# A two-layer decoder on one core: the last pairs of tiles of layer 2's expert loop put under conditions, its attention biases computed earlier, queries scaled on eviction, the residual added in the matmul

## The chip, the core and the metric

The kernel runs on one core of one Trainium2 chip. The core has a matmul engine (PE, with its weight loads listed apart as PEld), a vector engine (DVE), an activation engine (ACT), GpSimd (POOL) and a sync engine (SP); each works through its own list of instructions in order. In this kernel SP issues all plain transfers, and POOL issues the indirect ones, which scatter rows to listed places in DRAM or add rows there. The metric is the device time of one execution in microseconds. A profile is one such execution, recorded by the hardware profiler.

## The reference

Two layers, each a cross-attention and a mixture of experts, over x of 8 x 256 tokens of width 256 (2048 tokens), with a context of 8 x 120 rows:

```python
x = x + L0_xattn(layernorm(x), ctx, ctx, mask, w_q, w_k, w_v, w_o)      # 16 heads of 16, masked
x = x + L0_ffn(layernorm(x), ...)       # 64 experts, 8 per token, at most 128 tokens each, and a shared one
x = x + L1_xattn(layernorm(x), ctx, W_q, b_q, W_k, b_k, W_v, b_v, W_o, b_o)   # no mask, biases
x = x + L1_ffn(layernorm(x), ...)       # 32 experts, 6 per token, no limit; a shared one; 16 anchors
...
_, topidx = jax.lax.top_k(masked, TOP_K)                # 6 of 32 experts, from 2 of 4 groups
lg = topidx[:, 0] // (E // L)                           # one of 16 anchors, from the first expert
routed = jnp.einsum('te,teh->th', cw, eo)               # each expert: silu(x g) * (x u), then down
out = routed + shared + ANCHOR_ALPHA * anchor
```

Scores are divided by 4, the root of the head size. How many tokens fall to an expert or an anchor of layer 2 depends on the data; nothing limits it.

## The kernel before

**Order.** The program is unrolled. Attention and routing are written as tasks with an engine, an estimated duration and what they read and write; a planner (`Plan.run`) picks the task that can start first by its own estimates, with a rank, and so fixes each engine's list when the program is built. The expert loops (`expert_pairs`) are written out in a fixed order, with leftover tasks of the plan put between them (`beside`) in layer 1. Every engine instruction of these goes through the helper at L61, so the profile's groups have this line and are told apart by their tiles.

**Layer 1** runs attention and routing interleaved (two tiles of 128 tokens a unit of routing); POOL scatters each token's row to the lists of its 8 experts (`rows_f`, L237). Then 32 pairs of experts run: load the rows (`xg`), transpose (`xgp`), gate and up (`eg`), down (`eo`), weighting on ACT (`ye`), and POOL adds each half-pair to one of three accumulators in DRAM (`acc_f`, in the helper at L61). The experts' weights come in groups of four, six groups in buffers (`NEW`, L46).

**Layer 2's attention** begins at L328 with its biases: three small loads (`bc`, `br`, `bv`), the key bias split by the two halves of the heads (`bk`), and the value bias carried through the output weights (`bvs`, `bvp`) into `br`. Keys (`keys`, L357) and values (`values`, L376) are computed for all batches; each PSUM result is evicted in two parts, one by DVE and one by ACT, into KT and V. Then per pair of token tiles: `fetch` (L1229) loads layer 1's three partial sums and DVE adds them to x (`x_sb<-x_sb,sum_acc_f`), `queries` (L391) normalises, transposes and projects, and POOL adds `br` to x. Per tile `unit` (L422) computes the scores of 8 heads at a time; DVE takes the maxima and multiplies them by -0.25 (`mx_a<-mx_a`); ACT computes exp(0.25 s + m); PE transposes, weights the values, projects (`pj`); DVE adds the projection to x. Layer 1's units are the same with a mask, which DVE applies first (`pr_a<-sc_a,topm`).

**Layer 2's experts.** Tokens are sorted into tiles of 128 rows while routing runs: an expert gets a new tile whenever its last is full (`tiles`, L1040), so an expert with n tokens holds n/128 tiles, rounded up, numbered without gaps. `ntile` has each expert's count of tiles, and `own` which expert has which tile. There is room for 128 routed and 32 anchor tiles (L32), the most that can be needed. `ffn1` (L1116) goes through them in pairs, the 16 pairs of anchor tiles first, then the 64 routed pairs, all of them whatever the data: a tile that no expert took holds blank rows, is worked through with expert 0's weights, and its rows are added to spare rows of the accumulators. The number of each tile's expert is read from `which` into a register of PE. Last, `collect` (L269) loads the three accumulators by pieces of 256 tokens, DVE adds them to x, and SP stores the result.

**Buffers that tie this.** SP runs five pairs ahead with the rows; `yring` (L1128) holds four weighted pairs until their adds have landed, so ACT waits for adds and POOL for ACT.

Of the kernel before, what the change touches and what calls it, by code (L numbers as in the profile page):

```python
# [34 lines left out]
EPS = 1e-5  # L35
MASKED = -4.0e9
PAD = -3.0e38
# [7 lines left out]
EARLY = 2  # L45
NEW = 6  # L46
NRING = 7
NACC = 3

# [116 lines left out]
def decoder_kernel(ctx: ExitStack, tc: tile.TileContext, x, ctxT, mask, aw0, aw1, bqk, bvo,  # L166
# [20 lines left out]
    w_a0 = attention_weights(0, aw0)  # L187
    mi = const.tile([P, 2, SK], I32, tag="mi", name="mi")
    nc.sync.dma_start(mi, mask.rearrange("(t p) k -> p t k", p=P))
# [15 lines left out]
    nc.vector.tensor_reduce(par, hm.rearrange("p (q two) -> p two q", two=2), AX.X, ALU.add)  # L205

    side = const.tile([P, 2, QR], F32, tag="side", name="side")
    nc.vector.memset(side, 0.0)
    for q in range(2):
        nc.vector.memset(side[:, q, q * DH : (q + 1) * DH], 1.0)  # L210
    before = const.tile([P, P], F32, tag="before", name="before")
# [106 lines left out]
    def attention(layer, w, route, share):  # L318
# [9 lines left out]
        if layer:  # L328
            bc = w1.tile([P, 2, KD], F32, tag="bc", name="bc")
            nc.sync.dma_start(bc, bqk)  # L330

            bk = w1.tile([P, KD, 2], F32, tag="bk", name="bk")
            vector.tensor_tensor(bk, bc[:, 1].unsqueeze(2).to_broadcast([P, KD, 2]),
                                 par.unsqueeze(1).to_broadcast([P, KD, 2]), ALU.mult)
            br = w1.tile([P, D], F32, tag="br", name="br")
            nc.sync.dma_start(br, bvo[1:2, :].partition_broadcast(P))
            bv = w1.tile([P, KD], F32, tag="bv", name="bv")
            nc.sync.dma_start(bv, bvo[0, :].rearrange("(k p) -> p k", p=P))

            bvs = w1.tile([P, KD, P], F32, tag="bvs", name="bvs")  # L340
            vector.tensor_copy(bvs, bv.unsqueeze(2).to_broadcast([P, KD, P]))
            ps = ps_m.tile([P, D], F32, tag="m", name="bvp")
            for k in range(KD):
                tensor.matmul(ps, bvs[:, k, :], w[:, 3, k, :], start=(k == 0), stop=(k == KD - 1))
            vector.tensor_tensor(br, br, ps, ALU.add)
        else:
            m01 = w1.tile([P, 2, SK], F32, tag="m01", name="m01")
            vector.tensor_scalar(m01, mi, 0.0, None, ALU.not_equal)

            top = w1.tile([P, 2, SK], F32, tag="top", name="topm")  # L350
            vector.tensor_scalar(top, m01, BIG, MASKED, ALU.mult, ALU.add)

# [4 lines left out]
        def keys(m, c, rank):  # L357
            ps = m_tile([P, HB], f"kp_{n}_{m}_{c}")

            def product():  # L360
                for k in range(KD):
                    ins = tensor.matmul(ps(), w[:, 1, k, m * P : (m + 1) * P], cT[:, k, c * HB : (c + 1) * HB],
                                        start=(k == 0), stop=(k == KD - 1))
                return ins
            add("PE", 1.7, product, [], [ps], rank)
            dst = lambda q: KT[:, m, q, c * HB : (c + 1) * HB]
            bias = lambda q: bk[:, m, q : q + 1] if layer else 0.0
            add("DVE", 0.8, lambda: vector.tensor_scalar(dst(0), ps(), par[:, 0:1], bias(0), ALU.mult, ALU.add),
                [ps], [("K", layer, m, 0, c)], rank)
            add("ACT", 0.75, lambda: scalar.activation(dst(1), ps(), AF.Identity, scale=par[:, 1:2], bias=bias(1)),  # L370
                [ps], [("K", layer, m, 1, c)], rank)

# [3 lines left out]
        def values(b, rank):  # L376
# [7 lines left out]
            add("PE", 0.9, product, [], [ps], rank)  # L384
            for q, (e, copy) in enumerate((("DVE", vector.tensor_copy), ("ACT", scalar.copy))):
                split = lambda q=q: ps().rearrange("p (m c q d) -> p m q c d", m=KD, q=2, d=DH)[:, :, q]
# [4 lines left out]
        def queries(b, rank):  # L391
# [16 lines left out]
            def out_():  # L408
                if not layer:
                    return scalar.copy(QT(), ps())  # L410
                for m in range(KD):
                    ins = scalar.activation(QT()[:, m, :], ps()[:, m, :], AF.Identity, bias=bc[:, 0, m : m + 1])
                return ins
# [8 lines left out]
        def unit(i, QT):  # L422
# [3 lines left out]
            for half in range(2):  # L426
# [23 lines left out]
                def maxima(sc=sc, pr=pr, mx=mx):  # L450

                    if layer:
                        vector.tensor_reduce(mx().rearrange("p (c h) -> p c h", c=2), sc(), AX.X, ALU.max)
                    else:
                        vector.tensor_reduce(mx(), pr(), AX.X, ALU.max)
                    return vector.tensor_scalar(mx(), mx(), -0.25, None, ALU.mult)
                add("DVE", 1.32, maxima, [ps if layer else pr], [mx], i)
                pT = plan.tile(w2, [SK, 8, P], "pT", f"pT_{n}_{i}_{half}", 4)
                pTs.append(pT)
                for a in range(2):  # L460
                    c = 2 * half + a

                    def exponentials(sc=sc, pr=pr, mx=mx, a=a, c=c):

                        for h in range(4):
                            head = (h // 2) * HH + 2 * c + h % 2
                            to = pr()[:, 4 * a + h, :]
                            ins = scalar.activation(to, sc()[:, a, h, :] if layer else to, AF.Exp, scale=0.25,
                                                    bias=mx()[:, 4 * a + h : 4 * a + h + 1], accum_out=den()[:, head : head + 1])
# [40 lines left out]
            pj = m_tile([P, D], f"pj_{n}_{i}")  # L510

            def project():
                for k in range(KD):
                    ins = tensor.matmul(pj(), oT()[:, k, :], w[:, 3, k, :], start=(k == 0), stop=(k == KD - 1))
                return ins
            add("PE", 0.85, project, [oT], [pj], i - 0.5)
            add("DVE", 0.42, lambda: vector.tensor_add(x_sb[:, i, :], x_sb[:, i, :], pj()), [pj], [("x", i)], i - 0.5)

# [264 lines left out]
    def ffn0():  # L783
        stack = ExitStack()
        pool = lambda name, bufs, **kw: stack.enter_context(tc.tile_pool(name=f"f0{name}", bufs=bufs, **kw))
        w2, w3 = pool("b2", 2), pool("b3", 5)
        ps_g, ps_o = (pool(f"ps_{c}", 2, space=PSUM) for c in "go")
# [37 lines left out]
        def beside(s):  # L825
            plan.some(4)

        expert_pairs(0, list(range(E0 // 2)), (ps_g, ps_o), load, take,
# [23 lines left out]
    rt0 = f0.enter_context(tc.tile_pool(name="rt0", bufs=2))  # L852
    stack = attention(0, w_a0, route0, shared0)
    plan.run(lambda t: t.late < 1)
    stack.close()
# [260 lines left out]
    def ffn1():  # L1116
# [17 lines left out]

        pe = ps_m.tile([1, NTL], F32, tag="m", name="pe1")
        tensor.matmul(pe, wcol, own, start=True, stop=True)
        which = rt1.tile([1, NTL], I32, tag="ch1", name="which")
        vector.tensor_copy(which, pe)
# [62 lines left out]
        def actT_of(p):  # L1201
            o = 2 * P * (p % 2)
            return aring[0 : width(p), o : o + 2 * P].rearrange("p (j c) -> p j c", j=2)

        expert_pairs(1, [*range(NPR, NPR + NPA), *range(NPR)], (ps_g, ps_o), load, take,
                     lambda p: tring[:, p % 2], si_of, act_of, actT_of, gate_up, down_of, width, finish, lambda s: None, NRING - 2,
                     lambda t, g: scalar.activation(t, g, AF.Silu), False)

# [98 lines left out]
```

## Time and profile before

| | us |
|---|---|
| median of three runs (lowest, highest) | 1100.41 (1093.51, 1100.88) |
| the profiled execution | 1098.8 |
| its span, first to last instruction | 1097.1 |
| busy: PE, POOL, DVE, ACT | 851.0, 637.8, 572.2, 474.4 |
| last scatter of layer 1 issued | 263.7 |
| last add of layer 1's loop issued | 435.6 |
| first scores of layer 2 | 463.2 |
| last scatter of layer 2 issued | 741.5 |
| first and last add of layer 2's loop | 755.7, 1062.9 |

The span in 40 slices of 27 us (each digit the busy share in tenths):

```profile
PE   6989997997997782797979795507988899898710
PEld 4767775786996671565857674306776777777600
DVE  5988885752543341698766856503333433333305
ACT  3987785710231221296957380002333433343310
POOL 2047755564455677342505573673878888887860
PEclk9999996998999896898978986558999999999955
```

Read it by stages: to slice 10 layer 1's attention and routing, to 16 its experts, to 25 layer 2's attention and routing, then PE stops while POOL scatters, and from 28 on layer 2's experts. A busy engine isn't yet the one that sets the time: what counts is which wait ends last in each stage. In the tables by group a row has line, engine, operation, output and inputs, count, then total and mean time, and the idle time before them with what ended it.

### The profile page before, as it was taken

The page shows a single profiled execution, that of the slowest core. Times are in us where ns is not written, and L with a number is a line of the kernel's source. Part 1 is how long each engine was busy: PE and PEld are TensorE (multiplying, and loading weights), DVE is VectorE, ACT ScalarE, POOL GpSimd, SP SyncE. Part 2 cuts the span into 40 slices and gives each one's busy share as a digit, 9 for nine tenths or more (in the row PEclk, how much of TensorE's full clock was granted, in tenths as well). Part 3 has the DMA queues.
Part 4 walks back from the last instruction along what each step waited for, and adds up shares of the span by engine and source line. Part 5 has one row for each costly group of instructions (what it writes and reads, how often), then busy time and mean ns, then how long its engine had stood idle before and what let it go on. Part 6 is the DMA issues. An engine that isn't in the chain of part 4 may idle for free. (4 is left out here: it accounts for less than half of the span.)

```text
span 1097.1 us, 18163 instructions
## 1 busy us (share of the span) xinstructions
PE 851.0 (78%) x5630; PEld 685.5 (62%) x5630; DVE 572.2 (52%) x2025; ACT 474.4 (43%) x1756; POOL 637.8 (58%) x574
## 2 busy tenths in 40 slices
PE   6989997997997782797979795507988899898710
PEld 4767775786996671565857674306776777777600
DVE  5988885752543341698766856503333433333305
ACT  3987785710231221296957380002333433343310
POOL 2047755564455677342505573673878888887860
PEclk9999996998999896898978986558999999999955
DMA  9999999983699977630102222957978888888568
GB/s 319 298 353 277 275 286 257 348 305 97 170 285 324 241 126 105 172 108 30 58 1 72 83 98 103 405 222 199 166 137 145 145 147 147 146 153 137 68 98 270
DMA packets 158509, 202.34 MB, mean 184 GB/s; under 512 B 22343, under 2 KB 139406, under 8 KB 158160
## 3 DMA queue, kind: packets, MB, share of 16 engines
q1 hardware_dynamic: 114640, 144.86, 43.8%
q0 software_dynamic: 43776, 56.33, 28.9%
q8 instruction: 47, 0.77, 0.3%
q14 instruction: 46, 0.38, 0.1%
HBM read 95.19 MB, written 116.63 MB: 193 GB/s over the span
## 5 line engine op out<-in xcount | busy, mean ns | idle before, releaser
L237 POOL DMA_INDIRECT rows_f<-pay,idx x240 | 235.4, 981 | 192.3 <-issue 53.2
L61 POOL DMA_INDIRECT acc_f<-yring,etok x160 | 249.9, 1562 | 73.0 <-ACT yring L61 31.1
L61 POOL DMA_INDIRECT acc_f<-ye,etok x64 | 98.9, 1545 | 70.4 <-ACT ye L61 43.2
L61 ACT ACTIVATE yring<-eo,ewt 128x256 f32<-128x256 f32 x128 | 60.7, 475 | 152.7 <-DMA acc_f<-yring,etok 136.7
L61 PE MATMUL eg<-w,free 128*128 x512 | 121.5, 380 | 0.0
L61 DVE TENSOR_TENSOR free<-sring,eg 128x256 f32<-128x256 f32 (+1 forms) x80 | 31.6, 394 | 169.9 <-ACT sring L61 169.9
L61 ACT ACTIVATE pr_a<-pr_a,mx_a 128x120 f32<-128x120 f32 x256 | 97.9, 392 | 3.2 <-DVE mx_a L61 3.0
L61 PEld LDWEIGHTS eg<-w,free 128*128 128x128 f32 x512 | 92.8, 191 | 10.1
L61 ACT ACTIVATE pr_a<-sc_a,mx_a 128x120 f32<-128x120 f32 x256 | 90.9, 416 | 15.9 <-DVE mx_a L61 15.9
L61 PE MATMUL sc_a<-KT_a,QT_a 32*128 32x240 f32 x512 | 76.0, 427 | 16.1 <-ACT pr_a L61 9.2
L61 PE MATMUL tp_a<-ident,pr_a 128*120 128x128 f32 x512 | 82.9, 293 | 4.9 <-ACT pr_a L61 2.0
L61 ACT COPY pT_a<-tp_a 120x512 f32<-120x512 f32 x128 | 74.0, 614 | 23.9 <-PE tp_a L61 22.9
L61 DVE COPY free<-xgp 128x512 f32<-128x512 f32 x80 | 54.8, 685 | 50.0 <-PE xgp L61 49.8
L61 PE MATMUL xgp<-ident,room 128*128 128x128 f32 x320 | 50.6, 282 | 34.7 <-DMA room<-rows_f 34.5
L61 PEld LDWEIGHTS tp_a<-ident,pr_a 128*120 128x120 f32 x512 | 63.8, 146 | 21.5 <-ACT pr_a L61 10.7
L61 PE MATMUL eo<-w,aring 128*128 x256 | 68.7, 392 | 1.0 <-ACT aring L61 1.0
L61 PEld LDWEIGHTS xgp<-ident,room 128*128 128x128 f32 x320 | 39.8, 145 | 47.0 <-DMA room<-rows_f 34.9
L61 PEld LDWEIGHTS sc_a<-KT_a,QT_a 32*128 32x128 f32 x512 | 47.5, 206 | 33.2 <-ACT pr_a L61 16.1
L61 ACT ACTIVATE ye<-eo,ewt 128x256 f32<-128x256 f32 x64 | 26.9, 471 | 95.2 <-DMA acc_f<-ye,etok 64.6
L61 PE MATMUL eg<-xgT,ew 128*128 128x128 f32 x512 | 67.5, 289 | 0.0
L61 PEld LDWEIGHTS eg<-xgT,ew 128*128 128x128 f32 x512 | 65.4, 207 | 0.2
L61 ACT ACTIVATION_READ_ACCUMULATOR pr_a<-sc_a,mx_a 128x1 f32 x256 | 65.2, 262 | 0.0
(227 smaller groups left out, 1716.6 us busy)
## 6 DMA issues: line engine op xcount, KB each, us to landing
ew<-in_ew SPq DMA_DIRECT2D x16, 1536.0 KB, 9.1
rows_f<-blank SPq DMA_DIRECT2D x5, 4624.0 KB, 46.7
room<-rows_f SPq DMA_DIRECT2D x80, 289.0 KB, 3.5
acc_f<-blank SPq DMA_DIRECT2D x6, 2176.0 KB, 23.2
w<-in_ew SPq DMA_DIRECT2D x8, 1536.0 KB, 19.5
rows_f<-blank SPq DMA_DIRECT2D x2, 5136.0 KB, 44.9
xg<-rows_f SPq DMA_DIRECT2D x32, 321.0 KB, 6.2
sum_acc_f<-acc_f SPq DMA_DIRECT2D x24, 256.0 KB, 2.8
```

What stands on the lines that cost most here:

```text
L61: ins = call(*args, **kw)
L237: ins = nc.gpsimd.indirect_dma_start(out=rows, out_offset=bass.IndirectOffsetOnAxis(ap=idx, axis=0), in_=pay, in_offset=None, **kw)
```

## The change

Six edits. (1) `ffn1` runs 56 routed and 12 anchor pairs always; the rest stands in five blocks under nested conditions (two blocks of two anchor pairs; routed blocks of two, two and four), each entered if the count of tiles in use exceeds what has been worked through. The counts are sums of `ntile` by a matmul next to `pe1`, copied into `which`, and each engine reads them into a register. The blocks call `expert_pairs` anew. (2) Layer 2's biases are loaded during layer 1 into a buffer that the mask leaves free, and computed in step 24 of layer 1's expert loop. (3) Queries are multiplied by 0.25 as they are evicted, in both layers, so that the maxima are negated within the reduction and the multiplication after it falls away. (4) Layer 2's keys and values are evicted by ACT alone. (5) Layer 2's residual is added in PE by an identity matmul into the projection's PSUM, and ACT copies the sum to x; before, DVE added. (6) `NEW` goes from 6 to 7, the two pools of layer 1's loop change places in memory, and an unused constant (`side`) goes.

```diff
+SCALE = 0.25
-MASKED = -4.0e9
+MASKED = -1.0e9
-NEW = 6
+NEW = 7
+SURE = 56, 12
+LEFT = (2, 2, 4), (2, 2)
...
         if layer:
-            bc = w1.tile([P, 2, KD], F32, tag="bc", name="bc")
-            nc.sync.dma_start(bc, bqk)
...
+            bc, bk, br = consts1
...
-            add("DVE", 0.8, lambda: vector.tensor_scalar(dst(0), ps(), par[:, 0:1], bias(0), ALU.mult, ALU.add),
-                [ps], [("K", layer, m, 0, c)], rank)
...
+            for q in range(2):
+                if q or layer:
+                    add("ACT", 0.75, lambda q=q: scalar.activation(dst(q), ps(), AF.Identity, scale=par[:, q : q + 1], bias=bias(q)),
+                        [ps], [("K", layer, m, q, c)], rank)
...
-                    ins = scalar.activation(QT()[:, m, :], ps()[:, m, :], AF.Identity, bias=bc[:, 0, m : m + 1])
+                    ins = scalar.activation(QT()[:, m, :], ps()[:, m, :], AF.Identity, scale=SCALE, bias=bc[:, 0, m : m + 1])
...
-                        vector.tensor_reduce(mx().rearrange("p (c h) -> p c h", c=2), sc(), AX.X, ALU.max)
...
-                    return vector.tensor_scalar(mx(), mx(), -0.25, None, ALU.mult)
+                        return vector.tensor_reduce(mx().rearrange("p (c h) -> p c h", c=2), sc(), AX.X, ALU.max, negate=True)
+                    return vector.tensor_reduce(mx(), pr(), AX.X, ALU.max, negate=True)
...
             def project():
+                if layer:
+                    tensor.matmul(pj(), ident, x_sb[:, i, :], start=True, stop=False)
                 for k in range(KD):
...
+            if layer:
+                add("PE", 1.3, project, [oT, ("x", i)], [pj], i - 0.5)
+                add("ACT", 0.4, lambda: scalar.copy(x_sb[:, i, :], pj()), [pj], [("x", i)], i - 0.5)
+            else:
...
-        w2, w3 = pool("b2", 2), pool("b3", 5)
+        w3, w2 = pool("b3", 5), pool("b2", 2)
...
             plan.some(4)
+            if s == 24:
+                biases()
...
+    nc.sync.dma_start(bc, bqk)
+    nc.sync.dma_start(br, bvo[1:2, :].partition_broadcast(P))
+    nc.sync.dma_start(bv, bvo[0, :].rearrange("(k p) -> p k", p=P))
+
+    def biases():
+
+        vector.tensor_tensor(bk, bc[:, 1].unsqueeze(2).to_broadcast([P, KD, 2]),
+                             par.unsqueeze(1).to_broadcast([P, KD, 2]), ALU.mult)
+        vector.tensor_scalar(bc[:, 0], bc[:, 0], SCALE, None, ALU.mult)
...
+        vector.tensor_copy(bvs, bv.unsqueeze(2).to_broadcast([P, KD, P]))
+        ps = ps_m.tile([P, D], F32, tag="m", name="bvp")
+        for k in range(KD):
+            tensor.matmul(ps, bvs[:, k, :], w_a1[:, 3, k, :], start=(k == 0), stop=(k == KD - 1))
+        vector.tensor_tensor(br, br, ps, ALU.add)
...
+        pe = ps_m.tile([1, NTL + 2], F32, tag="m", name="pe1")
+        tensor.matmul(pe[:, 0:NTL], wcol, own, start=True, stop=True)
+        tensor.matmul(pe[:, NTL : NTL + 2], ntile, kind[:, 0 : NC1 : E1], start=True, stop=True)
...
-        expert_pairs(1, [*range(NPR, NPR + NPA), *range(NPR)], (ps_g, ps_o), load, take,
...
+        def pairs(*order):
+            expert_pairs(1, order, (ps_g, ps_o), load, take, lambda p: tring[:, p % 2], si_of, act_of, actT_of, gate_up,
+                         down_of, width, finish, lambda s: None, min(len(order), NRING - 2),
+                         lambda t, g: scalar.activation(t, g, AF.Silu), False)
...
+        in_use = [nc.values_load(which[0:1, NTL + c : NTL + c + 1], min_val=0, max_val=m, skip_runtime_bounds_check_because="a count")
+                  for c, m in ((0, NRT), (1, NAT))]
+        pairs(*range(NPR, NPR + SURE[1]), *range(SURE[0]))
+
+        def rest(c, p0, at, blocks):
+            if blocks:
+                with tc.If(in_use[c] > 2 * at):
+                    pairs(*range(p0 + at, p0 + at + blocks[0]))
+                    rest(c, p0, at + blocks[0], blocks[1:])
+
+        rest(1, NPR, SURE[1], LEFT[1])
+        rest(0, 0, SURE[0], LEFT[0])
```

## The prediction, made before the changed kernel ran

> **What bounds the kernel now.** I read the page first, then the busy time by stretches, then POOL's order of time in the last third, then the chain of waits, and last the gap between the layers. The page's chain and its two costliest groups there:
>
> ```profile
> DMA 17%; issue 6%; PE 4%; POOL 3%; DVE 1%; ACT 1%; SPq 0%; POOLq 0%; ACTq 0%; DVEq 0%
> L61 POOL DMA_INDIRECT acc_f<-yring,etok x160 | 249.9, 1562 | 73.0 <-ACT yring L61 31.1
> ```
>
> The chain consists mostly of the 160 indirect adds of layer 2's expert loop (80 pairs of tiles, two adds each). Is POOL, which issues them, the bound? The stretches (columns: stretch, its length, then busy time and count of PE, weight loads, DVE, ACT, POOL, then granted clock, DMA share, GB/s):
>
> ```profile
> 800.00:850.00 50.00, 42.63 (x223) 34.24 (x221) 17.33 (x84) 17.55 (x48) 39.45 (x26) 1.00 0.83 142
> 900.00:950.00 50.00, 46.09 (x246) 38.53 (x245) 19.23 (x92) 19.31 (x52) 40.84 (x27) 0.99 0.87 151
> 1050.00:1097.00 47.00, 0.00 (x0) 0.00 (x0) 16.43 (x24) 0.85 (x2) 12.30 (x8) 0.50 0.78 204
> ```
>
> POOL shows 82% busy and PE 92%, so PE looks nearer. The order of time on POOL says otherwise (start, duration, what, idle before it):
>
> ```profile
> 1059.13 1.57 POOL L61 DMA_INDIRECT acc_f<-yring,etok  x1 [0.30 <-issue]
> 1061.01 1.56 POOL L61 DMA_INDIRECT acc_f<-yring,etok  x1 [0.30 <-DMA acc_f<-yring,etok]
> 1062.87 1.57 POOL L61 DMA_INDIRECT acc_f<-yring,etok  x1 [0.30 <-issue]
> ```
>
> Each add takes 1.56 us and 0.30 us follows that nothing can use: a beat of 1.865 us, 3.73 us a pair. From 755.66 (first add) to 1064.44 (end of the last) are 308.8 us; 160 beats are 298.4. So only 10 us of the loop are not POOL's beat, and PE finishes at 1047.2, 17 us before POOL. The loop's length is the number of adds.
>
> After it the chain goes on through landing and collecting:
>
> ```profile
> 1061.01 1.56 POOL acc_f L61
> 1062.87 4.13 DMA acc_f<-yring,etok
> 1067.47 0.41 SPq L275
> ```
>
> The second place is the start of layer 2's attention. DVE there:
>
> ```profile
> 439.68 0.16 DVE L61 TENSOR_TENSOR bk<-bc,par 128x4 f32<-128x4 f32 x1 [19.81 <-DMA bc<-in_bqk]
> 442.26 0.47 DVE L61 COPY bvs<-bv 128x256 f32<-128x256 f32 x1 [2.42 <-DMA bv<-in_bvo]
> 445.17 0.42 DVE L61 TENSOR_TENSOR br<-br,bvp 128x256 f32<-128x256 f32 x1 [2.44 <-PE bvp L61]
> 448.59 0.78 DVE L61 TENSOR_SCALAR KT_a<-kp_a,par,bk 128x480 f32<-128x480 f32 x1 [3.01 <-ACT KT_a L61]
> 450.20 0.78 DVE L61 TENSOR_SCALAR KT_a<-kp_a,par,bk 128x480 f32<-128x480 f32 x1 [0.83 <-ACT KT_a L61]
> ...
> 451.10 0.68 DVE L61 TENSOR_TENSOR x_sb<-x_sb,sum_acc_f 128x512 f32<-128x512 f32 x1
> ```
>
> and PE, whose matmul before that ended at 421.11:
>
> ```profile
> 443.08 2.04 PE L61 MATMUL bvp<-w_a,bvs 128*128 128x256 f32 x4 [21.97 <-DVE bvs L61]
> ```
>
> The sums of layer 1's experts, issued from 439.31 and 2.8 us in flight, are on hand by about 442, but DVE, which works in program order, stands in the bias chain and the key evictions until 451.10.
>
> **The change, part by part.** *Pairs skipped.* The reference's routing on its inputs, counted per expert and rounded up to tiles of 128 rows, gives 112 routed tiles and 22 anchor tiles. The code always runs 56 and 12 pairs, so 112 and 24 tiles, and the conditions (over 112, over 24) are false: 8 routed and 4 anchor pairs go, 24 adds. At 1.865 us that is 44.8; with their share of the 10 us (24/160) it is 46.3. I take **-45**. The next limit, PE, needs about 3.4 us a routed pair (0.60 + 1.89 + 0.38 + 1.03 less overlap), under 3.73, so the beat stays POOL's.
>
> *Conditions.* Every engine loads two counts and jumps twice. The first count is read on POOL after its last scatter (741.5), where POOL idles 14.2 us; SP reads it after its 68 unconditional loads; ACT and DVE idle until 746. Nothing waits. At the loop's end it differs: in the built order POOL, on skipping, first waits until all earlier adds have landed, then raises the counters that the skipped adds would have raised, reads the second count, and does so again; SP's collecting loads queue behind that. Before, the loads of two accumulators left from 1062.99 and only the third waited for the last add. Now all seven of the first loads leave after the landing: 7 x 0.5 us = 3.6 after 1067, against 1069.4 before: +1.2. A register load or a jump has no row of its own. The nearest: PE's first gate group with two register loads took 2.04 us, later ones 1.06 with the loads run ahead, so at most 0.5 each. One read, two compares and two catch-ups on POOL: 0.5 to 3. From below no gain is excluded except by the landing itself, which is not shortened. Together **+3**, ends +1 and +10 (the far end is in a rival).
>
> The Trainium skill, "Runtime: NRT & Kernel Launch", section "Instruction fetch mechanics", speaks against this change: a taken jump to a target outside the two fetched blocks of 16 KiB stalls on a fetch. The page's code queue, 47 packets and 0.77 MB, agrees with blocks of that size; no jump is in this trace. The same skill's "Advanced Engine Details and Errata", section "Control Flow Timing", has about 0.1 us for a compare-and-branch, by which the term would stay under +2.
>
> *Biases early.* Three loads, four DVE operations and two matmuls leave the start of layer 2's attention. The loads go into SP's queue during layer 1's attention, ahead of the blank rows for layer 2, needed 400 us later; the compute sits in step 24 of layer 1's expert loop, DVE 0.16 + 0.17 + 0.47 + 0.42 and PE about 1 us. Step 24 lies near 390, in the stretch where POOL's adds run at their beat and PE waits for DVE and ACT, so this is free; uncovered it is 2.5 us, once. Keys and values no longer wait, and in the new order PE and ACT do the first ones between 421 and 438, while POOL issues the last adds of layer 1. ACT takes DVE's share, 4 x 0.75 + 8 x 0.27 = 5.2 us, on an ACT idle there for 20 us. POOL gets a value memset (0.5 us) ahead of its last add: +0.5. What remains for SP is the landing at 437.97, so the first sums leave 1.3 us earlier, the third lands near 442, and the third addition, now ended at 453.4, ends near 443: 10 us. From there to the first scores are 9.8 us (463.18), of which DVE's evictions and value copies take over 2. So 10 to 13; I take **-11**. If the sums land later than I think (their loads share the queue with anchor weights), 5 of it go.
>
> *Layer 2's attention itself.* DVE loses 16 residual adds (414 ns, 6.6 us) and 32 scalings of the maxima (180 ns, 5.8 us). PE gets 16 identity matmuls of 256 columns, half of a projection's 1.03 us: 8 us at most. ACT gets 16 copies at 431 ns: 6.9 us. From 470 to 500 all three are full (10.00, 9.5 and 9.96 of 10 us), from 520 to 610 mostly PE, in the routing stretches (510 to 520, 610 to 630, 660 to 670) DVE. With half of each exposed: -6 on DVE, +3.5 on PE. I take **-2.5**, ends -10 and +10: the order of the whole stage is planned anew.
>
> *Layer 1's attention* sheds 32 scalings (188 ns, 6.0 us) from a DVE that is busy 41 and 43.5 of 50 us; PE is at 45 and 46. Half: **-3**, ends 0 and -6. The queries' scale rides in an eviction that exists; the dropped setup operations lie before the first input lands. *A seventh weight buffer* sends one 1.5 MB load ahead of the loop; the loop's second half is POOL's adds, of which 15.4 us waited for DMA: **-1**, ends -4 and +3.
>
> Sum: -45 + 3 - 11 - 2.5 - 3 - 1 = -59.5. The profiled execution took 1098.8 us (span 1097.1 and 1.7 around it); that gives 1039.3. The median of the three runs is 1.6 above it: **1041**.
>
> **Rivals.** *Jumps that cost.* If each of POOL's four jumps fetched its code with the latency of a small DMA (1.6 us for the 2 KB bias load, 3.4 for the 1 KB one), and SP then did the same behind it, the term is +6 to +17 in place of +3: 1044 to 1055. For it: the skipped code lies inline. Against it: POOL's skipped code is only 24 issues, and SP and PE arrive early enough to hide theirs.
>
> *Work moved to the wrong engine.* PE is full in half of attention 2, ACT in its first 30 us; if their 8 and 7 us count in full and DVE's relief nothing, attention 2 loses 15 where I had 2.5 gained: 1058. For it: the full stretches. Against it: PE's waits in this stage name DVE results in seven of eleven rows.
>
> *Blocks that run*, the case on the other side, which is also the change not doing what it says. The condition is strict and 112 is the edge: one tile more and a block of two pairs runs. It can't overlap its neighbours: from the first load to the first add the loop took 11.8 us (743.84 to 755.66), plus the beats, 11.8 + 7.5 = 19.3, and 26.7 for four pairs. All five: 4 x 19.3 + 26.7 = 104, which gives 1145, slower by 4%. Three blocks (58) eat the whole gain; from the fourth it is slower. Against it: the nearest expert below a multiple of 128 needs 18 more tokens (238 to 256), far more than rounding moves.
>
> **How the numbers follow.** Forecast 0.74, costly jumps 0.10, attention loses 0.10, blocks run 0.04; 0.02 for a gain over 75. The forecast's own ends: loop -42 to -47, conditions +1 to +6, start -5 to -13, the attentions +4 to -14, weights +3 to -4, which don't all fall on one side: 1027 to 1056. The first two rivals reach to 1058, so the range is 1026 to 1060. A measurement of this kernel can tell about 1%, 11 us, from no change. Faster by more: 0.94; within: 0.03; slower: 0.03.
>
> **What would show it.** The adds of layer 2's loop number 136, at a beat of 1.86 us, and last about 263 us; none belongs to pairs 56 to 63 or 76 to 79. Between the last landing and the first collecting load stand 1 to 3 us. PE has key products before POOL's last add of layer 1, and the first addition of sums starts 3 to 5 us after that add has landed. The scalings of maxima are gone, and attention 2 from first scores to last scatter is about as long as now (463 to 741). I am wrong if the beat changes with fewer adds, if any conditional pair shows, or if that stage grows by over 10 us.

## The result, and the profile after

The changed kernel takes 1047.80 us (median of 4 runs, 1043.46 to 1050.70) against 1100.64 for the kernel before; the ratio is 0.954, interval 0.948 to 0.959. The forecast was 1041, range 1026 to 1060. The profiled execution took 1050.6 us, span 1048.8, which is 48.3 less than the span of before; the medians differ by 52.8.

I cut the span at six instants that every trace of this study shows: the end of layer 1's last scatter, the start of the last add of layer 1's loop, the first scores of attention 2, the end of the last scatter, the first and the last add of layer 2's loop. Each number is a difference of two start or end times in the order of time (us):

```text
stage                                     before  changed  difference  forecast
A  start to last scatter of layer 1        263.7    262.6     -1.1       -3
B  to last add of layer 1's loop           170.4    165.7     -4.7       -1
C  to first scores of attention 2           29.1     21.6     -7.5      -11
D  to last scatter (attention 2)           278.3    282.3     +4.1       -2.5
E  to first add of layer 2's loop           14.2     14.1     -0.1        0
F  to last add                             307.2    261.8    -45.4      -45
G  to the end                               34.2     40.6     +6.4       +3
```

Stage F is the one that pays. The group of the page that answers to the 160 adds of before (line, engine, operation, tiles, count, then busy time and mean ns, then idle time before them):

```profile
L64 POOL DMA_INDIRECT acc_f<-yring,etok x136 | 212.1, 1559 | 65.5 <-issue 22.6
```

24 adds fewer and the same 1.56 us each: no conditional pair ran. The order of time across the end of that loop, where the conditions stand (start, duration, engine and line, what, idle before):

```profile
1006.36 1.55 POOL L64 DMA_INDIRECT acc_f<-yring,etok  x1 [0.31 <-issue]
1008.21 1.56 POOL L64 DMA_INDIRECT acc_f<-yring,etok  x1 [0.30 <-issue]
1015.15 3.52 SPq L273 DMA_DIRECT2D room<-acc_f  x7
1018.07 1.49 DVE L64 TENSOR_TENSOR x_sb<-x_sb,room 128x512 f32<-128x512 f32 x2 [31.12 <-DMA room<-acc_f]
```

The beat is still 1.86 us. But the collecting loads, of which before had two in flight from 1062.99, next to its last add, now all leave 6.9 us after the last add started. SP's row in before:

```profile
1062.99 6.43 SPq L275 DMA_DIRECT2D room<-acc_f  x7
```

The sequencers' own rows for the conditional line say what lies between (queue, operation, count, shortest/median/longest ns, first and last start in us):

```profile
L1234 SPq COMPARE_BRANCH  x2: 45/48/50, 955.4 to 956.6; - x2
...
L1234 PEldq COMPARE_BRANCH  x2: 257/2098/3939, 990.5 to 993.2; - x2
...
L1234 POOLq COMPARE_BRANCH  x2: 45/49/53, 1006.9 to 1013.5; - x2
L1234 POOLq INC_SWDGE_SEM  x2: 873/886/900, 1012.2 to 1014.0; - x2
```

POOL's sequencer takes its first branch while the last adds are still queued (1006.9); then it waits for the last landing (1012.2), raises the counters for the skipped adds (0.9 us), reads the second count (0.3), branches (0.05) and raises again (0.9): with the gaps between these, 2.9 us until SP's first load, all in series. SP, DVE, ACT and PE had jumped long before, so theirs cost nothing (ACT's last branch starts at 998.0, 10 us before the last add).

At the start of attention 2, PE has key and value products before POOL's last add of layer 1 (428.24), and the sums are added as they land:

```profile
414.62 3.38 PE L64 MATMUL kp_a<-cT,w_a 128*128 128x480 f32 x8
...
428.57 3.57 PE L64 MATMUL kp_a<-cT,w_a 128*128 128x480 f32 x4 [6.14 <-ACT V_a L64]
```

```profile
435.68 1.48 DVE L64 TENSOR_TENSOR x_sb<-x_sb,sum_acc_f 128x512 f32<-128x512 f32 x2 [20.27 <-DMA sum_acc_f<-acc_f]
```

DVE no longer stands in the bias chain: from the start of the last add of layer 1 to the first addition of sums were 17.0 us (434.05 to 451.10), now 7.4 (428.24 to 435.68).

Two stages did not do what was forecast: A gained little and D grew. In layer 1's attention POOL's queue holds a copy that waits for a buffer whose rows are still being scattered (POOL's order of time):

```profile
84.19 0.97 POOL L235 DMA_INDIRECT rows_f<-pay,idx  x1 [0.54 <-ACT pr_a L64]
93.60 0.18 POOL L64 COPY pay<-tokid 128x2 int32<-128x2 int32 x1 [8.44 <-DMA rows_f<-pay,idx]
...
169.94 0.19 POOL L64 COPY pay<-tokid 128x2 int32<-128x2 int32 x1 [5.84 <-DMA rows_f<-pay,idx]
```

In before all four late copies of this kind stand behind the first 64 scatters, and only the last waits:

```profile
155.03 0.56 POOL L61 COPY pay<-tokid 128x2 int32<-128x2 int32 x3
...
162.36 0.19 POOL L61 COPY pay<-tokid 128x2 int32<-128x2 int32 x1 [6.78 <-DMA rows_f<-pay,idx]
```

In the changed order the first copy is drawn ahead, behind 16 scatters, at a time when the 16 DMA engines are full (share 1.08 between 80 and 100). A scatter takes 8.4 us to land there (the median in before from 60 to 160). POOL works in order, so the scatters and the power of the next normalisation stand behind the copy; DVE waits 7.5 us for the power and PE 7.5 us for DVE. Yet in this pair of traces A is no longer for it (262.6 against 263.7); the experiments come back to that.

In attention 2 a single wait of 9 us is seen on PE. The three engines there, in order of time:

```profile
539.31 1.08 PE L64 MATMUL sc_a<-KT_a,QT_a 32*128 32x240 f32 x8
549.35 1.97 PE L64 MATMUL sc_a<-KT_a,QT_a 32*128 32x240 f32 x8 [8.96 <-ACT pr_a L64]
```

```profile
546.45 0.36 ACT L64 ACTIVATE pr_a<-sc_a,mx_a 128x120 f32<-128x120 f32 x1 [6.61 <-DVE mx_a L64]
```

```profile
540.21 0.46 DVE L64 MAX8 top<-mk 128x8 f32<-128x32 f32 x4
...
545.26 2.21 DVE L64 TENSOR_REDUCE mx_a<-sc_a 128x8 f32<-128x960 f32 x2
```

Both score tiles are ready by 540.4. DVE first does a routing chain of 5 us, drawn ahead of them, and only then the two maxima; ACT and PE stand idle meanwhile.

### The profile page after: what moved, and what is told of

Read it like the earlier page. It is cut to its first block, busy times and chain, and to the rows that moved or that the text cites. A ratio compares the mean times of both kernels' runs of the same rounds, so it can differ in the third digit from the quotient of the medians.

```text
span 1048.8 us, 17459 instructions
## 1 busy us (share of the span) xinstructions
PE 816.8 (78%) x5448; PEld 657.1 (63%) x5448; DVE 539.9 (51%) x1863; ACT 466.6 (44%) x1736; POOL 599.9 (57%) x550
## 5 line engine op out<-in xcount | busy, mean ns | idle before, releaser
L64 POOL DMA_INDIRECT acc_f<-yring,etok x136 | 212.1, 1559 | 65.5 <-issue 22.6
L64 ACT ACTIVATE yring<-eo,ewt 128x256 f32<-128x256 f32 x112 | 53.1, 474 | 134.3 <-DMA acc_f<-yring,etok 116.9
L64 PE MATMUL eg<-w,free 128*128 x448 | 106.0, 379 | 0.0
L64 DVE TENSOR_TENSOR free<-sring,eg 128x256 f32<-128x256 f32 (+1 forms) x68 | 27.0, 397 | 139.5 <-ACT sring L64 139.4
L64 PEld LDWEIGHTS eg<-w,free 128*128 128x128 f32 x448 | 80.8, 190 | 8.7
L64 PE MATMUL sc_a<-KT_a,QT_a 32*128 32x240 f32 x512 | 72.0, 407 | 14.7 <-ACT pr_a L64 11.0
L64 DVE COPY free<-xgp 128x512 f32<-128x512 f32 x68 | 46.6, 685 | 50.0 <-PE xgp L64 50.0
L64 PE MATMUL xgp<-ident,room 128*128 128x128 f32 x272 | 42.4, 280 | 35.0 <-DMA room<-rows_f 35.0
L64 PE MATMUL gu<-xT_f,sw 128*128 128x256 f32 x256 | 61.7, 386 | 0.0
L64 PEld LDWEIGHTS xgp<-ident,room 128*128 128x128 f32 x272 | 33.5, 143 | 44.8 <-DMA room<-rows_f 35.4
```

Of the source, the lines that this page charges most:

```text
L64: ins = call(*args, **kw)
```

## Experiments

My theory after the first trace: the terms of the change add up, the loop carries nearly all, and attention 2 is longer because the residual (identity product on PE, copy on ACT) loads engines that are full there. The rivals: the loop's gain belongs in part to other edits; the conditions cost more than the gap shows; and, for attention 2, that not the load but the order that the planner draws is what counts. The kernels of one group ran on one chip and share the runs of before.

### The two halves of the change

**Conditions alone.** The kernel before, with this added:

```diff
+NRING = 7; SURE = 56, 12; LEFT = (2, 2, 4), (2, 2)
-        pe = ps_m.tile([1, NTL], F32, tag="m", name="pe1")
+        pe = ps_m.tile([1, NTL + 2], F32, tag="m", name="pe1")
+        tensor.matmul(pe[:, NTL : NTL + 2], ntile, kind[:, 0 : NC1 : E1], start=True, stop=True)
-        expert_pairs(1, [*range(NPR, NPR + NPA), *range(NPR)], ...
+        pairs(*range(NPR, NPR + SURE[1]), *range(SURE[0]))
+        rest(1, NPR, SURE[1], LEFT[1])
+        rest(0, 0, SURE[0], LEFT[0])
```

> The kernel before, with only the counting and the conditional blocks of the change. If the terms add up as forecast: the front is as before (first addition of the loop at about 755.7 us), the loop loses 24 adds x 1.865 us = 45, and the end pays 3.6 us for the conditions as the changed kernel's trace shows it: -41, about 1059 us. If the 2.8 us by which the changed kernel's collecting stage was longer belong to the conditions as well: -38, about 1062. Rival (the conditions also delay work ahead of the loop, since the count is read into registers there): the first addition of the loop comes later than 757 us.

**Everything but the conditions:** all 80 pairs in the loop again, no count.

> The changed kernel with all 80 pairs in the loop and without count and conditions. If the terms add up: -9.3 us as the front of the changed kernel shows it, the loop again 160 adds in about 309 us, about 1091 us; first addition of the loop at about 746.4. Rival (a part of the loop's gain of 45 belongs to the other edits): below 1088. Rival (the front's gain is given back behind it): about 1100.

**The 68 pairs, without count and blocks:**

```diff
-        pairs(*range(NPR, NPR + SURE[1]), *range(SURE[0]))
-        rest(1, NPR, SURE[1], LEFT[1])
-        rest(0, 0, SURE[0], LEFT[0])
+        expert_pairs(1, [*range(NPR, NPR + SURE[1]), *range(SURE[0])], ...
```

> The changed kernel with the 68 pairs in the loop and nothing conditional: no count, no blocks. It leaves out the pairs whose tiles are blank for these inputs, so it would be wrong for inputs that fill them. This measures what the conditions cost as a whole: 3.6 us less than the changed kernel, about 1044, if only the stretch from the last addition to the collecting stage pays for them; 6.4 us less, about 1041, if the longer collecting stage is theirs too; under 1 us less if neither is (then that stretch has another cause).

**One block that runs:**

```diff
-SURE = 56, 12
-LEFT = (2, 2, 4), (2, 2)
+SURE = 54, 12
+LEFT = (2, 2, 2, 4), (2, 2)
```

> The changed kernel with 54 routed pairs in the loop and a first conditional block of two pairs, which runs for these inputs (112 tiles in use, 108 handled before it). The forecast priced a block of two pairs that runs at 19.3 us where two pairs within the loop take 7.5: +11.8 us against the changed kernel, about 1060. Rival (code fetch of a block that runs costs as much as a drain): +20 or more, about 1068. Rival (engines run into the block without draining, since only registers are compared): +1 to +4, about 1050.

Measured (us; before on this chip 1093.54):

```text
kernel              median   ratio (interval)           A      C      D      F      G
conditions alone    1046.26  0.958 (0.952 to 0.964)   254.9   29.0  278.2  256.1  40.3
all but conditions  1092.78  0.997 (0.993 to 1.001)   260.5   22.0  285.0  304.3  35.7
68 pairs, static    1042.30  0.952 (0.946 to 0.958)   260.0   20.9  286.2  258.9  35.8
one block runs      1050.16  0.962 (0.955 to 0.968)   261.6   20.9  286.3  260.3  38.4
```

The conditions alone give 4.2%; with the changed kernel's 4.6% the intervals overlap. That is 46 us where I had expected 41. The loop of this trace is shorter than I had assumed: beside 135 beats of 1.865 us it has 4 us more, where before has 11 beside its 159 beats. All the other edits together give 0.3%, with no change inside the interval: about 3 us by the ratio, 0.8 by the medians, where I had forecast 17.5. Set against the conditions alone, the columns say why: C falls by 7 to 8 us, and D grows by 7 to 8 and A by 5 to 7. The rival "given back behind it" is nearer than my sum.

G separates by whether there are blocks: 34.2, 35.7 and 35.8 in the three kernels without; 38.9 to 40.6 in the ten profiled here and below whose blocks are all skipped. The means are 35.2 and 39.9, so the conditions cost 4.7 us. Of these, 3.7 lie between the last add and the first collected addition (5.1 to 6.9 us without blocks, 9.3 to 9.9 with them). Whether the rest, in the collecting stage, is theirs stays open: from the first collected addition to the end are 28.9, 30.6 and 28.8 us without blocks and 29.4 to 31.1 with them.

The block that runs is far cheaper than I had priced it. POOL there:

```profile
997.78 1.56 POOL L64 DMA_INDIRECT acc_f<-yring,etok  x1 [0.30 <-issue]
1004.00 1.55 POOL L64 DMA_INDIRECT acc_f<-yring,etok  x1 [4.66 <-ACT yring L64]
```

The hole is 4.66 us in place of 0.30, so two pairs in a block take 7.5 + 4.4 = 11.9 us, not 19.3: SP had read the count some 55 us earlier (its first branch in this kernel starts at 945.3) and had the block's rows loaded by then. The hole is mostly not the price of the block but that of the skip ahead of it, since the two anchor blocks are skipped first. The conditional line's rows on POOL's sequencer between 990 and 1006:

```profile
L1234 POOLq EVENT_SEMAPHORE  x3: 43/43/4661, 997.0 to 1001.7; - x3
L1234 POOLq INC_SWDGE_SEM  x1: 820/820/820, 1001.8 to 1001.8; - x1
```

The sequencer waits from 997.0 until the add of 997.78 has landed, raises the counters of the skipped anchor adds, reads the second count, and only then branches into the block (1003.1). These are steps that the changed kernel takes at its end, and G is 1.5 us shorter here (38.4 against a mean of 39.9). In all the kernel takes 7.9 us more than the static one by the medians, of which 4.7 are the conditions, so the rival of +1 to +4 us came nearest. What a block costs that follows another block that runs was not measured.

### Undoing single edits

**The residual on DVE again:**

```diff
-                if layer:
-                    tensor.matmul(pj(), ident, x_sb[:, i, :], start=True, stop=False)
-                add("ACT", 0.4, lambda: scalar.copy(x_sb[:, i, :], pj()), [pj], [("x", i)], i - 0.5)
+            add("DVE", 0.42, lambda: vector.tensor_add(x_sb[:, i, :], x_sb[:, i, :], pj()), [pj], [("x", i)], i - 0.5)
```

> The changed kernel with layer 2's residual on DVE again (the identity product on PE and the copy on ACT are undone). If the move of the residual is what made attention 2 longer by 4 us where 2.5 less was forecast: attention 2 (first scores to first scatter behind the idle before the last 42) falls from 224.7 to 218 to 221 us, about 1042 to 1044 in all. Rival (the two evictions of keys and values put on ACT did it): no change here, and a gain without them. Rival (the scaled maxima gave nothing and nothing here costs): all within 1 us.

**Keys and values evicted by DVE and ACT again:**

```diff
-            for q in range(2):
-                if q or layer:
-                    add("ACT", 0.75, ...
+            add("DVE", 0.8, lambda: vector.tensor_scalar(dst(0), ps(), par[:, 0:1], bias(0), ALU.mult, ALU.add), ...
+            add("ACT", 0.75, lambda: scalar.activation(dst(1), ps(), AF.Identity, scale=par[:, 1:2], bias=bias(1)), ...
```

> The changed kernel with layer 2's evictions of keys and values shared between DVE and ACT again. If ACT is what attention 2 waits for: 3 to 6 us less than the changed kernel (ACT gives back 0.75 x 64 key evictions in part), about 1043. If it is the residual's way through PE and ACT: within 1 us. If DVE is the bound of that stage: 2 to 5 us more.

**Biases late:** loads and chain at the start of attention 2 again, the rest as changed.

> The changed kernel with layer 2's biases loaded and worked out at the start of attention 2 again. The forecast gave them 11 us together with the whole start of attention 2, the trace of the changed kernel shows 7.5: 6 to 9 us more than the changed kernel, about 1055, first scores of attention 2 later by as much. Rival (the start of attention 2 came earlier because key products went ahead of the last additions, for another reason than the biases): under 2 us more.

**Six weight buffers, pools in the old order:**

```diff
-NEW = 7
+NEW = 6
-        w3, w2 = pool("b3", 5), pool("b2", 2)
+        w2, w3 = pool("b2", 2), pool("b3", 5)
```

> The changed kernel with six weight buffers and the pools of layer 1's pair loop in their old order. Layer 1's loop lost 4.7 us where 1 was forecast. If the seventh buffer is the cause: 3 to 5 us more than the changed kernel, last addition of layer 1 at about 432 to 433 instead of 428.2, about 1052. If it was the earlier start of that loop or the biases' place in it: within 1 us.

This chip was a slower one, 1143.97 us for before, and the changed kernel itself was not run on it; these four are compared with each other.

```text
kernel            median   ratio (interval)           B      C      D      F      G
residual on DVE   1079.29  0.943 (0.938 to 0.947)   168.8   21.5  298.9  258.6  40.1
K/V shared        1080.54  0.944 (0.939 to 0.948)   168.9   19.7  302.1  261.3  40.2
biases late       1088.44  0.951 (0.946 to 0.956)   166.0   21.8  306.6  259.2  39.1
six buffers       1090.42  0.952 (0.948 to 0.957)   164.9   19.8  308.6  258.6  40.1
```

Two expectations fell. With the biases late, C is 21.8, as in the changed kernel: the start of attention 2 did not come earlier through the early biases alone. SP issues the bias load at 425.91 there, ahead of the last add of layer 1 (450.45), and PE's keys follow at once (orders of time of SP and PE):

```profile
425.91 0.35 SPq L328 DMA_DIRECT2D bc<-in_bqk  x1
```

```profile
438.08 5.51 PE L64 MATMUL kp_a<-cT,w_a 128*128 128x480 f32 x8
```

In before that load left at 437.97, 3.9 us after the last add (434.05) started, and SP's waits name the landing of layer 1's adds (us in all, times, longest):

```profile
SPq L330 <- DMA acc_f<-ye,etok: 19.2, 5, 12.1
```

So its tile probably stood in memory that the loop's results still used, and edit (6), the swapped pools with the seventh buffer, changes what lies there; that is argued from the code. With edit (6) undone and the biases early, C is 19.8. So either edit is enough for this gain, and only without both (before, conditions alone) is C 29. The swap and the seventh buffer were not undone apart.

And six buffers leave B at 164.9: the 4.7 us of layer 1's loop are not the seventh buffer's. What they belong to was not found; in B the kernels with the changed attention code range from 164.6 to 168.9, those without from 170.4 to 171.0.

The residual and the key and value evictions looked like hits, 8 to 11 us by the medians against the two kernels below them in the table. They had to be checked beside the changed kernel.

### On one chip with the changed kernel

**The changed kernel again:**

> The changed kernel itself once more, so that it stands beside the other kernels of this call on one chip: ratio to before 0.949 to 0.959, with the stall of POOL behind the first scatters of layer 1 (7 to 8.4 us in the traces of the kernels with the same attention code) and one wait of PE's scores of about 9 us in attention 2.

**Both moves onto ACT undone** (the first two diffs of the group above together):

> The changed kernel with both the residual of layer 2 on DVE and the evictions of keys and values shared between DVE and ACT again; conditions, early biases, seventh buffer and scaled queries stay. If the two moves onto ACT are what lengthened attention 2 (5 to 8.6 us against before): 5 to 10 us less than the changed kernel of this call, attention 2 (second sum to last scatter) back at 289 us of the kernel before or below on a chip of its speed. Rival (what matters is the order that the planner draws, which any edit shuffles, and not ACT's load): no more than either move undone alone, or a loss.

**Six pay and idx buffers in layer 1:**

```diff
-        pay = plan.tile(rp0, [P, g, WX0], "pay", f"pay0_{i0}", 4)
+        pay = plan.tile(rp0, [P, g, WX0], "pay", f"pay0_{i0}", 6)
-        idx = plan.tile(rp0, [P, g, 8], "idx", f"idx_{i0}", 4, I32)
+        idx = plan.tile(rp0, [P, g, 8], "idx", f"idx_{i0}", 6, I32)
```

> The changed kernel with six buffers in place of four for layer 1's pay and idx tiles. If POOL's wait for a buffer whose scatters have not landed holds layer 1's attention up: the wait of 7 to 8.4 us after the first 16 scatters is gone, layer 1's last scatter comes 4 to 8 us earlier than in the changed kernel of this call, and so does the end. Rival (the transfers that fill the DMA engines at that time set the pace of the scatters): the wait comes back a few scatters later, and the last scatter within 2 us of where it was.

```text
kernel            median   ratio (interval)           A      C      D      F      G
changed, again    1042.97  0.956 (0.951 to 0.962)   260.3   20.1  284.1  257.5  40.6
both undone       1045.80  0.958 (0.951 to 0.964)   263.1   19.1  283.2  260.9  39.3
six pay buffers   1035.20  0.951 (0.945 to 0.957)   253.2   21.7  279.0  258.6  40.2
```

With both moves undone attention 2 is as long as with them (283.2 and 284.1), and the whole is 2.8 us slower by the medians, where my theory wanted 5 to 10 us less. These are single traces: the kernel with six pay buffers has the changed kernel's attention 2 unaltered, and its D is 279.0. But 5 us and more off the median would have shown, so the load on PE and ACT is not what lengthens the stage; my theory falls. Why either move undone alone did better on the slower chip stays open.

Six buffers take 7.8 us off the median (the intervals of the two ratios overlap). In the two traces A falls by 7.0 as the theory says, but D falls by 5.1 too, which the edit doesn't touch, and E and C grow by 1.7 and 1.6. The mechanism is only half as expected: the later wait (5.84 us in the changed kernel) is gone, but the early one is still there, since with six buffers it is the seventh copy that is drawn behind the first 16 scatters:

```profile
83.84 0.97 POOL L235 DMA_INDIRECT rows_f<-pay,idx  x1 [0.30 <-issue]
92.16 0.18 POOL L64 COPY pay<-tokid 128x2 int32<-128x2 int32 x1 [7.34 <-PE tp_a L64]
```

The profile names PE as what ended this wait, but the copy starts 8.3 us after the last of the 16 scatters, about the time that one takes to land.

The count of such waits goes with A within the two chips of these groups: one in the kernel with the conditions alone (254.9) against two in the three others of that chip (260.0 to 261.6); on the other chip one (253.2) against two (260.3, and 263.1 with both moves undone). In the first pair it does not: one in before (263.7), two in the changed kernel (262.6). So a cost of 5 to 7 us is likely, not shown. Eight buffers were not tried.

### The order on DVE

The last kernel tests the reading of the 9 us wait: not the load, but DVE's order. Beside it, in another stage, stands the price of a pair.

```diff
-                add("DVE", 1.16, maxima, [ps if layer else pr], [mx], i)
+                add("DVE", 1.16, maxima, [ps if layer else pr], [mx], i - 6 if layer else i)
-SURE = 56, 12
-LEFT = (2, 2, 4), (2, 2)
+SURE = 56, 11
+LEFT = (2, 2, 4), (3, 2)
```

> The kernel with six pay buffers, and two edits more in other stages: in layer 2 the planner ranks the maxima of a tile six tiles earlier, so that DVE takes them ahead of a routing chain; and 11 anchor pairs in place of 12 stand outside the blocks (22 anchor tiles are in use). If DVE's order, routing chain before maxima that lie ready, is what makes PE wait 9 us at once in attention 2: that wait is gone and the stage (second sum to last scatter, 290.5 us with six buffers) takes 5 to 15 us less. Rival (the routing that is put off comes late instead, since it ends in the scatters that the loop waits for): within 2 us of 290.5, or longer. The loop in any case loses two adds x 1.865 = 3.7 us: 134 adds, no conditional pair. In all about 1022 us by the first, 1032 by the rival, on a chip on which the kernel with six buffers takes 1035.

This kernel does not compute pair 74, the last anchor pair, as the reference does: with an odd number of anchor pairs ahead, pair 74 and pair 0 follow each other with the same half of the two-half buffer for transposed rows, and by the code pair 0's rows are written there before pair 74's products read it. Stage D ends before that, and no instruction is left out.

It takes 1019.86 us, ratio 0.936 (0.933 to 0.938), on a chip on which before takes 1091.33. D is 263.9 against 279.0 with six buffers: 15 us less, the upper end of the expectation, out of one number in the planner. F is 254.6 against 258.6: 4.0 for the two adds, 3.7 expected. PE's two largest waits in attention 2, first with six buffers, then with the maxima first (who waits for whom, us in all, times, longest):

```profile
PE sc_a L64 <- ACT pr_a L64: 11.1, 4, 9.0
PE tr_f L64 <- DVE pay L64: 10.1, 3, 6.6
```

```profile
PE sc_a L64 <- ACT pr_a L64: 5.6, 5, 2.0
PE tr_f L64 <- DVE pay L64: 5.6, 2, 4.5
```

The wait of 9.0 us is gone, and the longest is 2.0. By these two rows PE waits 10 us less in all, of the 15. The longest wait alone does not tell: with both moves undone it is 5.6 us in place of 9.0, but PE's four waits for ACT there still sum to 11.3, and D stayed. The two traces are from two chips, but D in all kernels with the changed attention code was 279.0 to 286.3 wherever before takes 1093 to 1101 us. The kernel with the maxima first and 12 anchor pairs, which computes all, was not run; by the parts measured it should take some 4 us more than this one, which is argued, not shown. The fastest kernel here that computes everything is the one with six pay buffers. Whether before would gain as much from the same rank was not tried.

## Why the prediction was right where it was, and where it failed

**Pairs skipped (-45): right, with its reason.** -45.4, and 24 adds at the beat. That it agrees to half a microsecond is luck: in the kernels with 136 adds F is 256.1 to 261.8. The limit behind POOL did not show: with fewer pairs the beat stayed 1.86 us. The counts of tiles hold too, as far as the blocks tell: over 108 routed tiles and not over 112, and not over 22 anchor tiles (134 adds in the last kernel).

**Conditions (+3): right in mechanism, low in size.** 4.7 us by the means above, 6.4 between the two first traces, within +1 to +10. What I had short is the catch-up on POOL: two at 0.87 and 0.90 us where I had a register load's 0.5 as a bound for each. From the last landing to the first collecting load the whole takes 2.9 us, at the far end of my 1 to 3. The rival of costly jumps fails where I placed it: POOL's two branches take 45 and 53 ns. A jump that costs does exist, PE's second at 3.94 us, but PE was through with it at 997, 11 us before the last add started. The Trainium skill, "Runtime: NRT & Kernel Launch", section "Instruction fetch mechanics", says a taken jump out of the fetched window stalls on a fetch; PE's one row of 3.94 us fits that, the 45 to 72 ns on SP, ACT, DVE and POOL don't show it. The Trainium skill, "Advanced Engine Details and Errata", section "Control Flow Timing", gives about 0.1 us for a compare-and-branch: on those four engines the trace has 45 to 72 ns, about half of it, and the trace decides.

**Start of attention 2 (-11): right stage, too large, and half the wrong cause.** C fell by 7.5. The third sum is added 9.1 us sooner after the last add (19.3 to 10.2), the 10 that I had; but from there to the scores it takes 1.6 us longer, where I had added another 1. And the step "biases early" was not the only cause: edit (6), which I had costed under the weight buffer alone, frees the same wait.

**Attention 2 (-2.5): this step failed.** It became 4.1 us longer in the first pair of traces and 7 to 8 on the chip of the first group. I had taken half of each engine's change in load as exposed, and even so my sum had 3.5 us for half of PE's 8 and nothing for ACT's 6.9. DVE did lose the work: in stage D it is busy 167.3 us against 179.9 before. But the stage waits on orders rather than loads: both moves undone changed it by 1 us, one rank by 15. The ends that I gave the term (-10 to +10) held it, though my summary of the ends had only +4 to -14 for both attentions; the middle was worth nothing.

**Layer 1's attention (-3): the step failed in the same way.** -1.1 in the first pair, 5 to 7 longer on the chip of the first group. DVE is relieved, but the new order puts a copy that waits for landings early into POOL's queue, for 5.8 to 8.4 us of POOL's time at each of two places in the changed kernel; that this is what A pays is likely, not shown. I named the queues for the edits that move DMAs, and not for this stage, whose order I had seen would be planned anew.

**Weight buffer (-1): not the cause.** B fell by 4.7 with seven buffers and lies in the same place with six.

Of the -17.5 us forecast ahead of the loop, -9.3 came in the first pair (A to E), and 3 us, not distinguishable from none, on the chip where it was measured alone. The total stayed within the range because the loop is nine tenths of it; that the misses ahead of the loop and the dearer conditions together stayed under the 19 us up to the range's end was not foreseen. Of the rivals, work moved to the wrong engine had its 15 us nowhere, and a block that runs was priced at 19.3 us on the ground that it can't overlap its neighbours, where one took 11.9, most of its gap being the skip ahead of it. What all five would cost was not measured.

## What to carry to other kernels

Cost a skipped piece of work by the beat of the engine that sets the loop, and the jump by what has to be done in series after the last landing: here 45 us and 5. Where a planner lays out a stage, relieving an engine need not give anything by itself, and here it didn't; look for the instructions that stand in an in-order queue ahead of work that is ready, since moving those was worth 15 us where moving the residual additions and the evictions to other engines gave nothing that could be measured. When several edits free one wait, undo them singly and together before one of them is given the credit.

## What the runs showed of the hardware

- A compare-and-branch takes 38 to 72 ns on SP, ACT, DVE and POOL (changed kernel and the one whose block runs); on PE it took 257 and 3939 ns in the changed kernel, 70 to 3776 in the other.
- POOL's catch-up for skipped indirect adds takes 0.82 to 0.90 us each time, whether four or eight pairs were skipped, and comes after a wait for the adds before it to land.
- A count read from memory into a register takes 0.29 to 0.67 us in these two kernels; the second of two on one engine is not always the shorter.
- One kernel, before, has medians of 1091 to 1101 us in four groups of runs and 1144 on one chip. There attention 2 of the changed code takes 299 to 309 us in place of 279 to 286 and A 283 to 287 in place of 253 to 264, at granted clocks of 0.854 to 0.870 in place of 0.875 to 0.893, while the loop of adds is the same (258.6 to 261.3). So these stages were longer on that chip and the loop that POOL sets was not; why is open.
